# Layer 0 of a four-layer graph network on one core: input loads on one queue, row sums turned by transposes, four index searches moved behind the scaled rows

## The chip, the core and the metric

The kernel runs on 1 core of one Trainium2 chip, as one launch. The metric is device time in microseconds (us): three runs before the change gave a median of 1217.2 us, from 1211.95 to 1225.6. Engines are called PE (matmul), PEld (its weight loads), DVE (vector), ACT (scalar), POOL (GpSimd) and SP (sync, which here only issues transfers). A name with a q behind it, as in SPq, is the sequencer's own work of issuing.

## The reference, cut to what matters

There are 2708 nodes with 128 features `x` and a dense matrix `adj` of 2708 x 2708. Every layer is `x = x + layer(relu(layernorm(x)))`. The change lies in layer 0 (with small consequences in shared helpers):

```python
def layer0(h, A, W1, b1, W2, b2):           # h = relu(layernorm(x)), k = 4
    def lap_mul(A, x):
        d = 1.0 / sqrt(sum(A, axis=-1))     # row sums of A
        return d[:, None] * (A @ (d[:, None] * x))
    z  = leaky_relu(lap_mul(A, h) @ W1 + b1, 0.1)
    sq = sum(z * z, axis=-1)
    d2 = maximum(sq[:, None] + sq[None, :] - 2.0 * (z @ z.T), 0.0)
    S  = exp(-sqrt(d2 + 1e-10) / 2.0)
    S  = where(rank of S in its row < 4, S, 0.0)   # the four nearest nodes
    return lap_mul(S + A, h) @ W2 + b2
```

Layers 1 to 3 are a graph attention (done with a sort and tables), a mean over neighbours, and a plain graph convolution.

## The kernel before, in words

**Tiling.** The nodes lie in T = 22 tiles of 128 rows, the last with 20. `adjT` (the transpose of `adj`) comes from DRAM in 22 chunks of 128 rows x 2708 columns of float32, 1354 KB each; the last has 20 rows (211.6 KB). Columns are handled in six blocks `KBS`: five of 512 and one of 148. `GROUPS` are groups of four tiles, six in all. Chunks 0 to 16 rotate through the four buffers of the pool `big`; chunks 17 to 21 have buffers of their own (`res17` to `res21`) and stay resident between the row sums and the first product of layer 0. The instructions of each engine are put in order by the scheduler of the tile framework, apart from those wrapped in `pin`, which keep the program's order.

**Loads at the start.** ACT's queue loads the nodes `xs` (L85, L86), six weights (L90), three biases spread to all rows (L95), `a_nat` (L105) and stores `order_d` (L137). SP's queue loads the chunks of `adj` (L245). The framework gives the transfers of these hardware queues eight semaphores in turn, so that a transfer also waits for the one that had its semaphore before. The last chunk is loaded four times, to partitions 0, 32, 64 and 96, so that its matmuls with 20 rows can use four row groups of the array.

**Row sums.** As each chunk comes, L355 multiplies it with columns of ones: output in four column groups of 32, six matmuls (twelve instructions of PE, [...]). In between, `weighted` makes `h0 @ W1` and `h0 @ W2` (L323, L334, L341). The sums lie along rows; L372 turns them to one value per partition with 22 matmuls of one column each, and `evacuate` (L149 on DVE, L151 on ACT, in alternation) copies them to `degs`. `inv_sqrt` (L200, L202) makes `dinv`, and L191 scales `y1`.

**First product and z.** `aggregate(y1, to_z)` multiplies all chunks with `y1` (L267) into six PSUM banks `acc0` to `acc5`, the resident chunks last. For each group `to_z` turns the result (L222), makes z (L401, L411), squares it (L414), transposes it to `zT` (L211) and splits -sq/2 into three bf16 parts (L418 to L422), which L427 turns into three rows `sq_rows`.

**Strips.** For each tile t, L463 multiplies z with zT into the six banks, L469 adds the three rows `sq_rows` (a matmul with 3 rows of bf16), and ACT copies the banks to a strip of 128 x 2708 (L472). DVE finds the eight largest of each row (L474, `max`) and their places (L476, `max_index`). Strips use the four buffers of `big`. For the last two tiles the places are searched later, by `find_last` (L490).

**Similarities and second product.** L495, L499 (DVE), a square root and an exponential (L500, L501, ACT) give `sim`; then `find_last(T-2)`, `row_numbers` (L484 to L486), the new row sums (L505, L507), `dinv2` (L200, L202) and the scaled rows `y2` (11 tiles on DVE, L518, 11 on ACT, L516). Two stores write `y2` to `ydr` (L522). `find_last(T-1)` comes last. `aggregate(y2, to_x1)` runs the same products again. Beside it POOL gathers the rows of the four nearest nodes from `ydr` (L539, 88 gathers) and DVE adds them (L545).

Of the kernel before, what the change touches and what calls it, by code (L numbers as in the profile page):

```python
# [18 lines left out]
P = 128  # L19
# [6 lines left out]
def kernel(  # L26
# [44 lines left out]
    ps_a = ctx.enter_context(tc.tile_pool(name="ps_a", bufs=1, space=PSUM))  # L71


    ident = consts.tile([P, P], F32, name="ident")
# [7 lines left out]

    xs = keep.tile([P, T, D], F32, name="xs")
    nc.vector.memset(xs[:, T - 1, :], 0.0)
    nc.scalar.dma_start(xs[:, : T - 1, :], x[: (T - 1) * P, :].rearrange("(t p) f -> p t f", p=P))  # L85
    nc.scalar.dma_start(xs[:TAIL, T - 1, :], x[(T - 1) * P :, :])  # L86

    def load_w(name, w):
        t = consts.tile([P, P], F32, name=name)
        nc.scalar.dma_start(t, w)  # L90
        return t

    def load_b(name, b):
        t = consts.tile([P, P], F32, name=name)
        nc.scalar.dma_start(t, bass.AP(tensor=b.tensor, offset=b.offset, ap=[[0, P], [1, P]]))  # L95
        return t
# [7 lines left out]
    with nc.allow_non_contiguous_dma(reason="256 elements"):  # L104
        nc.scalar.dma_start(  # L105
            a_nat, bass.AP(tensor=l1_a.tensor, offset=l1_a.offset, ap=[[1, P], [P, 2]])
        )
# [28 lines left out]
    nc.vector.memset(nowhere[:, :, 1:2], -1e5)  # L136
    nc.scalar.dma_start(order_d.rearrange("(p t) c -> p t c", t=T), nowhere)  # L137

# [7 lines left out]
    def evacuate(dst, src):  # L146
# [3 lines left out]
        else:  # L150
            nc.scalar.copy(dst, src)  # L151

    def pin(ins):

        return tc.keep_in_program_order(ins)

# [74 lines left out]

    resident = {}
    pools = {}

    def chunk(i):
        if i in resident:
            return resident[i]
        if i >= T - pools["n"]:
            c = resident[i] = pools["res"].tile([P, N + 1], F32, name=f"res{i}")
        else:  # L240
            c = big.tile([P, N + 1], F32, name="chunk", tag="big")

        for g in range(4 if i == T - 1 else 1):
            pin(
                nc.sync.dma_start(  # L245
                    c[32 * g : 32 * g + width(i), :N], adjT[i * P : i * P + width(i), :]
                )
            )
        return c

    def spread(y, queue):

        for g in range(1, 4):
            queue.dma_start(y[32 * g : 32 * g + TAIL, T - 1, :], y[:TAIL, T - 1, :])

    def aggregate(y, done, more=None, kept=0):

        out = [acc(b) for b in range(NKB)]
        last = T - pools["n"]

        def product(i, b):
            k0, n = KBS[b]
            r = slice(32 * (b % 4), 32 * (b % 4) + TAIL) if i == T - 1 else slice(0, P)
            nc.tensor.matmul(  # L267
                out[b][:, :n],
                y[r, i, :],
                chunk(i)[r, k0 : k0 + n],  # L270
                start=(i == 0),
                stop=(i == T - 2),
            )

        for i in range(last):
            if more is not None:
                more(i)
            resident[i] = chunk(i)
            for b in range(NKB):
                product(i, b)  # L280
            if i < last - kept:
                del resident[i]
            if i % 2 and last + i // 2 < T:
                chunk(last + i // 2)
        if more is not None:
            for i in range(last, T):
                more(i)
        for b in range(NKB):
            product(T - 1, b)
        for b in range(NKB):  # L290
            for i in range(last, T - 1):
                product(i, b)
            if b:
                done(b - 1, out)
        done(NKB - 1, out)
# [5 lines left out]

    rows_open = ExitStack()
    res_rows = rows_open.enter_context(tc.tile_pool(name="rows", bufs=1))
    pools.update(res=res_rows, n=L0_RES)
    l0 = ExitStack()
# [42 lines left out]
    for i in range(T):  # L348
# [4 lines left out]
        for b, (k0, n) in enumerate(KBS):  # L353
            g = 32 * (b % 4)
            nc.tensor.matmul(  # L355
                sums[b // 4][g : g + 32, :n],
                ones[:w, :32],
                c[:w, k0 : k0 + n],
                start=(i == 0),
                stop=(i == T - 1),  # L360
            )
    sum_rows = lay.tile([P, 1024], F32, name="sum_rows", tag="U")
    for half, p0, p1 in ((0, 0, 128), (1, 0, 32 * (NKB - 5)), (1, 32 * (NKB - 5), 32 * (NKB - 4))):
        n = KBS[4 * half + p0 // 32][1]
        evacuate(sum_rows[p0:p1, 512 * half : 512 * half + n], sums[half][p0:p1, :n])

    pd = [acc(j) for j in range(4)]
    for b, (t0, t1) in enumerate(GROUPS):
        j = b % 4
        for t in range(t0, t1):  # L370
            o = 512 * (b // 4) + P * (t % 4)
            nc.tensor.matmul(  # L372
                pd[j][: width(t), t : t + 1],
                sum_rows[32 * j : 32 * j + 1, o : o + width(t)],
                ones[32 * j : 32 * j + 1, :1],
                start=True,
                stop=True,
            )
    for b, (t0, t1) in enumerate(GROUPS):
        e = min(t1, T - 1)  # L380
        evacuate(degs[:, t0:e], pd[b % 4][:, t0:e])
    evacuate(degs[:TAIL, T - 1 :], pd[(NG - 1) % 4][:TAIL, T - 1 : T])
    dinv = inv_sqrt("dinv", degs)
# [9 lines left out]

    parts = res.tile([P, T, 3], BF16, name="parts")
    rest = res.tile([P, T, 2], F32, name="rest")
    sq_rows = res.tile([3, N], BF16, name="sq_rows")
    nc.vector.memset(z[:, T - 1, :], 0.0)
# [7 lines left out]
    def to_z(g, s1):  # L405
# [6 lines left out]
        for t in range(t0, t1):  # L412
            junk = small.tile([P, D], F32, name="junk")
            nc.scalar.activation(junk, z[:, t, :], AF.Square, accum_out=sq[:, t, :])  # L414
        transposed(zT, z, g)
        r0, r1, r2 = sq[:, t0:t1, :], rest[:, t0:t1, 0:1], rest[:, t0:t1, 1:2]
        b0, b1_, b2_ = (parts[:, t0:t1, c : c + 1] for c in range(3))
        nc.vector.tensor_scalar(b0, r0, -0.5, None, op0=ALU.mult)  # L418
        nc.vector.scalar_tensor_tensor(r1, r0, -0.5, b0, op0=ALU.mult, op1=ALU.subtract)
        nc.vector.tensor_copy(b1_, r1)  # L420
        nc.vector.tensor_tensor(r2, r1, b1_, ALU.subtract)
        nc.vector.tensor_copy(b2_, r2)  # L422
        p = ps_s.tile([P, 512], F32, name="ps")
        for t in range(t0, t1):
            o = (t - t0) * P
            w = width(t)
            nc.tensor.matmul(  # L427
                p[:3, o : o + w], parts[:w, t, :], ident_b[:w, :w], start=True, stop=True
            )
        evacuate(sq_rows[:, span(g)], p[:3, : span(g).stop - span(g).start])  # L430

# [22 lines left out]
    top_v = res.tile([P, T, 8], F32, name="top_v")  # L454
    top_i = res.tile([P, T, 8], U32, name="top_i")
    strips = []
    nc.vector.memset(top_v[:, T - 1, :], 0.0)
    for t in range(T):
        w = width(t)
        s = big.tile([P, N + 1], F32, name="strip", tag="big")[:, :N]  # L460
        zz = [acc(b) for b in range(NKB)]
        for b, (k0, n) in enumerate(KBS):
            mm = nc.tensor.matmul(  # L463
                zz[b][:w, :n], zT[:, cols(t)], zT[:, k0 : k0 + n], start=True, stop=False
            )
            if t == 1 and b == 0:
                pin(mm)
        for b, (k0, n) in enumerate(KBS):
            nc.tensor.matmul(  # L469
                zz[b][:w, :n], ones_b[:3, :w], sq_rows[:, k0 : k0 + n], start=False, stop=True  # L470
            )
            nc.scalar.copy(s[:w, k0 : k0 + n], zz[b][:w, :n])  # L472
        strips.append(s)
        nc.vector.max(top_v[:w, t, :], s[:w, :])  # L474
        if t < T - 2:
            nc.vector.max_index(top_i[:w, t, :], top_v[:w, t, :], s[:w, :])  # L476


# [20 lines left out]
    pin(nc.vector.tensor_scalar(sim, sim, 0.0, None, op0=ALU.max))  # L499
    nc.scalar.activation(sim, sim, AF.Sqrt, bias=d2_eps)  # L500
    nc.scalar.activation(sim, sim, AF.Exp, scale=-0.5)  # L501
    find_last(T - 2)
    row_numbers(P, 0, T - 1)
    deg2 = small.tile([P, T, 1], F32, name="deg2")
    pin(nc.vector.tensor_reduce(deg2, sim, AX.X, ALU.add))  # L505
    deg2s = small.tile([P, T], F32, name="deg2s")
    pin(nc.vector.tensor_tensor(deg2s, deg2[:, :, 0], degs, ALU.add))  # L507
    dinv2 = inv_sqrt("dinv2", deg2s)
    y2 = lay.tile([P, T, D], F32, name="y2", tag="Y")
# [3 lines left out]
    for t0, t1 in ((0, T // 2), (T // 2, T)):  # L513
        for t in range(t0, t1):
            if t % 2:
                nc.scalar.mul(y2[:, t, :], hw2[:, t, :], dinv2[:, t : t + 1])  # L516
            else:
# [7 lines left out]
        )  # L525
    find_last(T - 1)
    row_numbers(TAIL, T - 1, T)
# [7 lines left out]
    def add_near(t, late=False):  # L535
        w = width(t)
        for k in range(TOPK):
            g = res.tile([P, D], F32, name="gath", bufs=24)
            nc.gpsimd.indirect_dma_start(  # L539
# [760 lines left out]
```

## Time and profile before

| what | us |
|---|---|
| runs, median (lowest to highest) | 1217.2 (1211.95 to 1225.6) |
| the profiled execution | 1218.29 |
| its span | 1216.2 |
| chunk sums end (last L355) | 91.2 from the span's start |
| first matmul of the first product | 97.6 |
| first `max` of the strips | 225.0 |
| last `max` of the strips ends | 347.4 |
| first matmul of the second product | 352.9 |
| layer 0 hands over to layer 1 | about 441 to 482 |

The profile lists, for each engine, what it ran and why it was idle before. A "stage" here is a stretch of the span in microseconds from its start. In the timeline a row is: start, length, engine, line, operation, output<-input, shape, number of merged instructions, and in brackets the idle time before it with what ended that. PE was busy 1054.7 us (87% of the span), DVE 563.8, ACT 407.5, POOL 237.0; the mean granted clock of PE was 0.928. These shares are averages over stages with different limits, so the stages are read one by one.

### The profile page before, as it was taken

Reading aid. Unit: us, or ns where it says so; the run is one execution under the profiler, and the core shown is the slowest. Engines: PE = TensorE matmul, PEld = TensorE weight load, DVE = VectorE, ACT = ScalarE, POOL = GpSimd, SP = SyncE. Lnnn points to the kernel's source line nnn. Section 1 sums busy time; section 2 is a strip of 40 time slices with the busy share of each in tenths; the row PEclk is TensorE's granted clock in tenths of the full one; section 3 lists DMA queues with packets and bytes.
Section 4 is the critical chain, followed back from the end, with each engine's and each line's share of the span. In section 5 each row is a group of like instructions: output and inputs, shape, how many; then the busy total and the mean of one; then the engine's idle time right before and its main releaser. Section 6 shows DMA issues by size and latency. Waiting matters only on the chain.

```text
span 1216.2 us, 10253 instructions
## 1 busy us (share of the span) xinstructions
PE 1054.7 (87%) x3637; PEld 507.0 (42%) x3637; DVE 563.8 (46%) x1172; ACT 407.5 (34%) x643; POOL 237.0 (19%) x200
## 2 busy tenths in 40 slices
PE   4889999999969996977787807777999999999998
PEld 0325444444424445543333303333454455545444
DVE  2001004899972357816666648999720040114003
ACT  3100003444430034767667436878600040003000
POOL 0200000000017773441111035866000000000000
PEclk8998999999989996978989857998889999999999
DMA  8997830000059823869999889999299807753831
GB/s 307 426 359 299 307 133 1 1 0 1 1 218 400 318 53 113 360 222 322 367 380 403 350 351 418 424 424 380 82 383 351 317 33 276 268 184 105 308 136 46
DMA packets 40160, 298.77 MB, mean 246 GB/s; under 512 B 7103, under 2 KB 11214, under 8 KB 13650
## 3 DMA queue, kind: packets, MB, share of 16 engines
q1 hardware_dynamic: 24076, 202.37, 44.3%
q0 software_dynamic: 13600, 93.75, 20.3%
q10 hardware_dynamic: 2434, 2.01, 0.6%
q8 instruction: 29, 0.48, 0.2%
q14 instruction: 21, 0.17, 0.0%
HBM read 265.76 MB, written 32.87 MB: 246 GB/s over the span
## 4 chain that ended last, share of the span: by engine, by line
PE 53%; DVE 20%; DMA 19%; issue 6%; POOL 1%; ACT 1%; SPq 0%; POOLq 0%; DVEq 0%; ACTq 0%
PE acc L267 40%; DMA mov<-in_adj_dram,src_u 7%; DVE top_v L474 5%; DMA chunk<-in_adj_dram 5%; DVE top_i L476 5%; DVE hi L1131 4%; DVE hi L1119 4%; DMA hi<-table,hi_u 2%; DMA res<-in_adj_dram 2%; PE ps L847 2%; PE acc L1036 2%; PE acc L1141 1%; PE ps L224 1%; DMA xs<-in_x_dram 1%; PE ps L355 1%
## 5 line engine op out<-in xcount | busy, mean ns | idle before, releaser
L1141 PE MATMUL acc<-hi,xw 128*128 128x512 f32 (+2 forms) x264 | 119.8, 612 | 63.2 <-DVE hi L1131 63.2
L267 PE MATMUL acc<-chunk,y 128*128 128x512 f32 (+1 forms) x408 | 159.3, 554 | 12.8 <-DVE y L518 10.7
L267 PE MATMUL acc<-chunk,h 128*128 128x512 f32 (+1 forms) x384 | 148.0, 542 | 0.0
L1036 PE MATMUL acc<-mov,wt 128*128 128x512 f32 (+1 forms) x264 | 119.7, 608 | 28.7 <-DMA mov<-in_adj_dram,src_u 28.7
L539 POOL DMA_INDIRECT gath<-ydr,near_u x88 | 84.4, 959 | 284.8 <-DMA ydr<-y 258.3
L267 PEld LDWEIGHTS acc<-chunk,y 128*128 128x128 f32 x408 | 75.0, 194 | 97.1 <-issue 85.6
L463 PE MATMUL acc<-zT 128*128 128x512 f32 (+2 forms) x264 | 108.2, 552 | 1.5 <-ACT strip L472 1.1
L1141 PEld LDWEIGHTS acc<-hi,xw 128*128 128x128 f32 (+1 forms) x264 | 53.7, 212 | 129.1 <-DVE hi L1131 66.7
L1040 DVE COPY mov<-acc 2x512 f32<-2x512 f32 (+1 forms) x126 | 74.6, 612 | 61.0 <-PE acc L1036 59.6
L267 PEld LDWEIGHTS acc<-chunk,h 128*128 128x128 f32 x384 | 68.8, 190 | 74.1 <-issue 74.1
L1036 PEld LDWEIGHTS acc<-mov,wt 128*128 128x128 f32 x264 | 52.5, 210 | 92.0 <-issue 78.0
L472 ACT COPY strip<-acc 128x512 f32<-128x512 f32 (+2 forms) x132 | 60.7, 558 | 73.5 <-issue 58.5
L267 PE MATMUL acc<-chunk,attended 128*128 128x512 f32 x192 | 76.9, 563 | 5.1 <-DMA chunk<-in_adj_dram 5.1
L463 PEld LDWEIGHTS acc<-zT 128*128 128x128 f32 (+1 forms) x264 | 46.4, 185 | 57.3 <-issue 34.1
L1073 POOL DMA_INDIRECT lo<-table,lo_u x22 | 56.0, 2547 | 71.5 <-DVE hi L1119 31.5
L1041 ACT COPY knots<-acc 128x512 f32<-128x512 f32 x88 | 49.9, 586 | 55.7 <-DVE mov L1040 40.0
L1119 DVE SCALAR_TENSOR_TENSOR hi<-lo,lam,hi 128x2708 f32<-128x2708 f32 (+4 forms) x25 | 67.2, 2697 | 1.0
L1123 ACT ACTIVATE hi<-hi,lam 128x2708 f32<-128x2708 f32 (+4 forms) x25 | 56.7, 2280 | 32.5 <-issue 23.4
L1131 DVE SCALAR_TENSOR_TENSOR hi<-row_all,inv_s,hi 128x2708 f32<-128x2708 f32 (+4 forms) x25 | 67.0, 2692 | 0.0
L474 DVE MAX8 top_v<-strip 128x8 f32<-128x2708 f32 (+1 forms) x22 | 64.3, 2963 | 0.2 <-ACT strip L472 0.2
L476 DVE FIND_INDEX8 top_i<-top_v,strip 128x8 uint32<-128x2708 f32 x20 | 59.2, 2972 | 0.0
L545 DVE SCALAR_TENSOR_TENSOR xs<-gath,simd,xs 128x128 f32<-128x128 f32 (+1 forms) x88 | 30.6, 351 | 59.9 <-DMA gath<-ydr,near_u 59.2
(270 smaller groups left out, 1168.1 us busy)
## 6 DMA issues: line engine op xcount, KB each, us to landing
chunk<-in_adj_dram SPq DMA_DIRECT2D x110, 1354.0 KB
table<-knots SPq DMA_DIRECT2D x20, 1354.5 KB
res<-in_adj_dram SPq DMA_DIRECT2D x9, 1354.0 KB
res<-in_adj_dram SPq DMA_DIRECT2D x8, 211.6 KB
ydr<-y SPq DMA_DIRECT2D x2, 704.0 KB
gath<-ydr,near_u POOLq DMA_INDIRECT x88, 5.5
chunkY<-in_adj_dram SPq DMA_DIRECT2D x1, 1354.0 KB
chunkU<-in_adj_dram SPq DMA_DIRECT2D x1, 1354.0 KB
```

The source lines that it names most:

```text
L267: nc.tensor.matmul(out[b][:, :n], y[r, i, :], chunk(i)[r, k0 : k0 + n], start=(i == 0), stop=(i == T - 2),)
L463: mm = nc.tensor.matmul(zz[b][:w, :n], zT[:, cols(t)], zT[:, k0 : k0 + n], start=True, stop=False)
L472: nc.scalar.copy(s[:w, k0 : k0 + n], zz[b][:w, :n])
L474: nc.vector.max(top_v[:w, t, :], s[:w, :])
L476: nc.vector.max_index(top_i[:w, t, :], top_v[:w, t, :], s[:w, :])
L539: nc.gpsimd.indirect_dma_start(out=g[:w, :], out_offset=None, in_=ydr[:, :], in_offset=bass.IndirectOffsetOnAxis(ap=near_u[:w, t, k : k + ...
L1036: nc.tensor.matmul(p[:, :n], wt[:, t, :], moving[t][:, k0 : k0 + n], start=True, stop=True)
L1040: nc.vector.tensor_copy(moving[t + 1][:2, k0 : k0 + n], p[:2, :n])
L1119: nc.vector.scalar_tensor_tensor(num, lo[:w, c], kap, num, op0=ALU.mult, op1=ALU.add)
L1123: nc.scalar.activation(num, num, AF.Ln, scale=sc)
L1131: nc.vector.scalar_tensor_tensor(att[:w, c], row_all[:w, c], inv_s[:w, t : t + 1], att[:w, c], op0=ALU.max, op1=ALU.mult,)
L1141: nc.tensor.matmul(py[b][:, :n], xw[:w, t, :], att[:w, k0 : k0 + n], start=(t == 0), stop=(t == T - 1),)
```

## The change

1. **Loads.** `xs` is loaded first on SP's queue, then chunk 0, the last 20 rows of `xs`, and chunks 1 to 3, and so on. The weights, biases, `a_nat` and `order_d` move from ACT's queue to POOL's. Chunk 21 is loaded once; its three further copies (`last_rows`) follow after four chunks of the first product have been asked for.
2. **Turning the row sums.** The 22 one-column matmuls become ten transposes: four of 128 columns x 128 rows for the first 16 tiles, then four and two on 32 rows. DVE alone copies the results to `degs`, four copies in place of seven.
3. **Squares in four row groups.** The three bf16 parts are written four times, 32 columns apart, so that `sq_rows` holds them at partitions 0, 32, 64 and 96; the 3-row matmul of block b uses row group b % 4, and each tile's blocks go in two batches, four and two.
4. **Index searches.** The searches of tiles 18 and 19 join those of tiles 20 and 21 behind the scaled rows. Strips 18 and 19 use buffers of other tiles (`U` and `Z` of the pool `lay`). `row_numbers` of tiles 0 to 17 comes before the last `max`.
5. **Functions.** The two square roots become exp(0.5 ln) and exp(-0.5 ln); the table of ACT with both is loaded after the copies of tile 4, and the square root's table again after the scaled rows.
6. **Scaled rows.** 13 tiles on DVE, 9 on ACT. The gather buffers go from 24 to 23.

```diff
+    def chunk(i):
...
+        pin(nc.sync.dma_start(c[: width(i), :N], adjT[i * P : i * P + width(i), :]))
+        if i == T - 1:
+            pools["apart"] = True
+        return c
+
+    def last_rows():
+        pools["apart"] = False
+        for g in range(1, 4):
+            pin(
+                nc.sync.dma_start(
+                    resident[T - 1][32 * g : 32 * g + TAIL, :N], adjT[(T - 1) * P :, :]
+                )
+            )
...
+    pin(nc.sync.dma_start(xs[:, : T - 1, :], x[: (T - 1) * P, :].rearrange("(t p) f -> p t f", p=P)))
+    FIRST = 4
+    for i in range(FIRST):
+        resident[i] = chunk(i)
+        if i == 0:
+            pin(nc.sync.dma_start(xs[:TAIL, T - 1, :], x[(T - 1) * P :, :]))
...
-    nc.scalar.dma_start(xs[:, : T - 1, :], x[: (T - 1) * P, :].rearrange("(t p) f -> p t f", p=P))
-    nc.scalar.dma_start(xs[:TAIL, T - 1, :], x[(T - 1) * P :, :])
...
-        nc.scalar.dma_start(t, w)
+        nc.gpsimd.dma_start(t, w)
...
             resident[i] = chunk(i)
+            if i > 2 and T - 1 in resident and pools["apart"]:
+                last_rows()
...
-    pd = [acc(j) for j in range(4)]
-    for b, (t0, t1) in enumerate(GROUPS):
-        j = b % 4
-        for t in range(t0, t1):
-            o = 512 * (b // 4) + P * (t % 4)
-            nc.tensor.matmul(
-                pd[j][: width(t), t : t + 1],
-                sum_rows[32 * j : 32 * j + 1, o : o + width(t)],
-                ones[32 * j : 32 * j + 1, :1],
...
+    for g0, g1 in [(0, 4)] + [(b, b + 1) for b in range(4, NKB)]:
+        pd = acc(max(g0 - 3, 0))
+        r0, r1 = 32 * (g0 % 4), 32 * (g0 % 4 + g1 - g0)
+        e = min(4 * g1, T)
+        for c in range(min(4, e - 4 * g0)):
+            w = min(width(4 * b + c) for b in range(g0, g1))
+            o = 512 * (g0 // 4) + P * c
+            nc.tensor.transpose(
+                pd[:w, P * c : P * c + r1 - r0], sum_rows[r0:r1, o : o + w], ident[r0:r1, r0:r1]
+            )
...
-    sq_rows = res.tile([3, N], BF16, name="sq_rows")
+    sq_rows = res.tile([P, N], BF16, name="sq_rows")
...
+        b0, b1_, b2_ = (part[:, :n, :, c] for c in range(3))
...
+        nc.vector.tensor_scalar(b0, four(r0), -0.5, None, op0=ALU.mult)
...
+    LATE = T - 4
...
+        for bs in (range(4), range(4, NKB)):
+            for b in bs:
+                k0, n = KBS[b]
+                mm = nc.tensor.matmul(
+                    zz[b][:w, :n], zT[:, cols(t)], zT[:, k0 : k0 + n], start=True, stop=False
+                )
...
+            for b in bs:
+                k0, n = KBS[b]
+                g = 32 * (b % 4)
+                nc.tensor.matmul(
+                    zz[b][:w, :n],
+                    ones_b[g : g + 3, :w],
+                    sq_rows[g : g + 3, k0 : k0 + n],
...
-        if t < T - 2:
+        if t < LATE:
             nc.vector.max_index(top_i[:w, t, :], top_v[:w, t, :], s[:w, :])
+        if t == 4:
+            with tc.issue_after(copied.ins):
+                nc.scalar.preload_act_table_set("natural_log_exp_and_others")
...
-    nc.scalar.activation(sim, sim, AF.Sqrt, bias=d2_eps)
+    nc.scalar.activation(sim, sim, AF.Ln, bias=d2_eps)
+    nc.scalar.activation(sim, sim, AF.Exp, scale=0.5)
     nc.scalar.activation(sim, sim, AF.Exp, scale=-0.5)
-    find_last(T - 2)
-    row_numbers(P, 0, T - 1)
+    row_numbers(P, 0, LATE)
...
-    dinv2 = inv_sqrt("dinv2", deg2s)
+    dinv2 = keep.tile([P, T], F32, name="dinv2")
+    nc.scalar.activation(deg2s, deg2s, AF.Ln)
+    nc.scalar.activation(dinv2, deg2s, AF.Exp, scale=-0.5)
...
-            if t % 2:
+            if t % 5 in (1, 3):
...
-    find_last(T - 1)
+    with tc.issue_after(scaled.ins):
+        nc.scalar.preload_act_table_set("sqrt_and_others")
+    for t in (T - 2, T - 1, *range(LATE, T - 2)):
+        find_last(t)
+    row_numbers(P, LATE, T - 1)
     row_numbers(TAIL, T - 1, T)
```

## The prediction

> **What bounds the kernel now.** I read the page's slices first (DMA runs at its height only early, PE later), then the busy times by stage, then inside each stage what ended the last wait. By stage (columns: PE, PEld, DVE, ACT, POOL busy, PE's clock, DMA share, GB/s):
>
> ```profile
> 12.00:15.00 3.00, 1.32 (x12) 0.12 (x2) 0.15 (x1) 0.00 (x0) 0.00 (x0) 1.00 0.96 246
> 27.00:81.00 54.00, 46.79 (x298) 19.14 (x302) 4.20 (x10) 9.65 (x23) 6.16 (x1) 0.97 1.01 424
> 81.00:91.00 10.00, 7.44 (x40) 1.59 (x32) 1.04 (x3) 0.00 (x0) 0.00 (x0) 0.83 1.01 226
> 225.00:342.00 117.00, 116.60 (x354) 51.12 (x353) 117.00 (x61) 53.20 (x118) 0.00 (x0) 1.00 0.02 7
> 342.00:353.00 11.00, 0.35 (x4) 0.09 (x1) 10.50 (x15) 5.99 (x13) 0.00 (x0) 0.66 0.44 186
> ```
>
> The row sums (to 91 us) are bound by DMA: 424 GB/s in mid-stage, but 246 while `xs` and weights come in short rows, and 226 at the end, where the last chunk comes four times. The strips (225 to 342) are bound by DVE, 117.00 us of 117, with PE at 116.60. Then PE waits 11 us. The issues and waits at the start:
>
> ```profile
> 0.82 0.88 SPq L245 DMA_DIRECT2D chunk<-in_adj_dram  x2
> 1.83 9.43 ACTq L86 DMA_DIRECT2D xs<-in_x_dram  x1
> 15.13 1.90 SPq L245 DMA_DIRECT2D chunk<-in_adj_dram  x2
> ...
> SPq L245 <- DMA w<-in_L_gnn_W_dram: 13.4, 1, 13.4
> ```
>
> SP issues two chunks at once and the third only at 15.13: it waits for a weight's transfer, whose semaphore it shares, though its buffer is free. The end of the strips:
>
> ```profile
> 330.35 4.81 PE L463 MATMUL acc<-zT 128*128 128x512 f32 x12
> 335.09 1.31 PE L469 MATMUL acc<-sq_rows,ones_b 3*128 3x512 bf16 x6
> 336.33 4.72 PE L463 MATMUL acc<-zT 128*20 128x512 f32 x12
> 341.44 2.67 ACT L472 COPY strip<-acc 20x512 f32<-20x512 f32 x6 [3.16 <-issue]
> 341.55 5.83 DVE L474 MAX8 top_v<-strip 128x8 f32<-128x2708 f32 x2
> 347.89 2.97 DVE L490 FIND_INDEX8 top_i<-top_v,strip 128x8 uint32<-128x2708 f32 x1
> 348.33 1.28 ACT L501 ACT_TABLE_LOAD   x1
> 349.91 1.28 ACT L200 ACT_TABLE_LOAD   x1
> 352.94 5.54 PE L267 MATMUL acc<-chunk,y 128*128 128x512 f32 x9 [10.65 <-DVE y L518]
> ```
>
> PE makes a strip in 5.98 us (330.35 to 336.33), DVE uses one in 5.83. The last strip is ready at 344.11 and wanted at 344.46: DVE gets no faster here by losing work alone. Then an index search and two table loads stand before the second product.
>
> [...] The trace has such a pack: twelve instructions of 20 rows at L267, 177.82 to 179.73, 1.91 us, against some 4.6 us for twelve of 128 rows. [...]
>
> **The change part by part** (times against the profiled span).
>
> 1. Loads. `xs` is 1.386 MB; first bytes flow at about 2.3 us (the first 3 us moved 0.27 MB). At 246 GB/s it takes 5.6 us, landing near 7.9 instead of 14.85. The eleven small loads, 0.59 MB, cost 2.4 us of DMA [...]. Chunks 0 to 20 are 21 x 1.387 MB at 424 GB/s, 68.7 us. SP no longer waits on weights: in the changed program's list the first wait for a semaphore is with chunk 4, on a transfer landed long before. So chunk 20 lands at 2.3 + 5.6 + 2.4 + 68.7 = 79.0, against 85.83: 6.8 us. Then before, two sums took 85.83 to 91.21, 5.4 us, [...] two take 2 x 1.9 = 3.8 us. End at 82.8, gain 8.4. I take 8.0, since one copy of 20 rows stays. Bounds: 3, if `xs` holds SP as it held ACT's queue (L86, 9.43 us) and transfers pause after it; 10, if short rows run faster alone. POOL's queue: weights stand before its iotas and L385, which was idle 28.8 us before; `w1` is wanted first by L334 at chunk 4. Nothing, unless over 10 us late. The three late copies, 2.8 us at 226 GB/s, stand before chunk 4 of the first product; PE uses 4.6 us a chunk, DMA brings one in 3.27: hidden.
>
> 2. Turning. Before: 91.21 to 97.61, 6.4 us, of which 4.25 in 44 instructions. After: copy of the sums by ACT (0.57), ten transposes (0.66 for four, as at L323, and some 0.6 for the rest), degs copies (0.16 each, two after the last transposes), DVE's 0.30 us copy of the sums' last block, then 0.2 + 0.7 + 0.3 + 0.7 for root, two reciprocals and first scaling, with gaps: 4.2 us. Gain 2.2 (1 to 3).
>
> 3. z stage. Part copies of 16 in place of 4 elements and matmuls 128 wide in place of 3: some 0.1 us a group, as 0.17 us is nearly all fixed cost. Alternation of evacuations flips, with no net load. The first strip gets its last block straight after the last `sq_rows` (in the new order only wg's transposes stand between), where before two L463 and a transpose came first (222.77 to 224.37): gain 1.2 (-1 to 2.5).
>
> 4. Strips. DVE: 22 max and 20 searches took 224.96 to 347.38, 2.915 us each. After: 22 and 18, 116.6, plus `row_numbers` 0.7 ahead of the last max: gain 5.1, if the strips come in time. They need PE below 5.98 - (344.11 - 224.96 - 114.4) / 21 = 5.755 us a strip (114.4 is when the last max is wanted: 39 x 2.915 + 0.7). L463 holds 4.74; two packs of bf16 matmuls cost 2 x 0.21 plus some 0.1 each of start, as the 1.91 us above [...] suggest, against 1.31; and the 0.27 us wait for ACT's first copy goes, as four banks are copied while the other two are filled. Estimate 5.5 (5.2 to 5.9). Strips 18 and 19 have own buffers, so PE is not held.
>
> 5. Chain. Before: 347.38 to y2 at 352.55, 5.2 us. After: 0.5 (L495, L499), ln 0.37, two exp 0.28, reduce and add 0.4, ln and exp 0.22 each, gaps: 2.6. Gain 2.6 (2 to 3). The table loads move beside copies (ACT 53.20 of 117 us busy).
>
> 6. Searches behind. With S the start of y2: DVE scales 13 rows at 0.2 (2.7), then four searches of 3.05: S + 14.9. Queued behind are `row_numbers`, `simd`, the adds L545 at S + 16.2. POOL's first gather waits for ydr and rows 0 to 17 alone (S + 8); at 1.25 us a gather, the 24th, first to need a buffer back, is at S + 36: covered. Chunk 2's load needs strip 20's buffer, free at S + 5.7 (before, issued at S + 3.7); with 3.3 us of transfer [...] it lands near S + 11, and PE wants it at 0.4 + 6.3 + 4.6 = S + 11.3. I charge 0.4 (0 to 2). DVE stays idle 59.9 us beside the gathers, so the adds catch up.
>
> Sum: 8.0 + 2.2 + 1.2 + 5.1 + 2.6 - 0.4 = 18.7 us. Gathers, second product and layers 1 to 3 shift as they are. The profiled execution, 1218.3, becomes 1199.6; it stood 1.1 above the median 1217.2, so the likeliest time is 1199.
>
> **The rivals.** (a) As worked out: 1199, chance 0.68; its own range is 1193 to 1204. (b) Packs don't overlap beside full-width float32: PE stays at 5.98, the last strip comes as before, part 4 gives 0.3: 1204. For: PEld sits idle 0.75 us after the 20-row pack. Against: the pack itself. Chance 0.13. (c) `xs` blocks SP's queue, part 1 gives 3: 1204; together with a late chunk 2, 1206. For: the 9.43 us issue. Against: ACT's queue had to share. Chance 0.11. (d) Slower: each change between full weights and row groups, four a strip, empties the array. Had each pack 0.76 us (the idle time PEld shows before such loads in the z stage), a strip would take 4.74 + 0.63 + 1.52 = 6.89 us, 21 x (6.89 - 5.755) = 24 us late: 1223. It decides from 6.65 us a strip (21 x 0.89 = 18.7). Against: L469 follows L463 today within 0.1 us. Chance 0.04. The remaining 0.04 lies below 1193: more of the first 27 us recovered.
>
> **How the numbers follow.** The range 1191 to 1207 holds (a) to (c). A measurement of this kernel can tell about 1% from no change: faster means under 1205.0. (a), the low rest, and most of (b) and (c): 0.86; within 1%: 0.10; slower 0.04.
>
> **What would show it.** Right: SP issuing chunk 2 in the first microseconds, chunk 20 near 79, L267 from about 87.5; strips at about 5.5 us of PE and DVE without gaps; no table load between the last max and y2, 2.6 us; PE's second product near 334. Wrong: DVE idle for strips; PE idle on chunk 2 after y2; row sums ending past 86.

## The result, and the profile after

The changed kernel takes 1200.5 us (median of 4 runs, 1196.96 to 1212.45); in the same runs the kernel before took 1216.9. The ratio is 0.986, 95% interval 0.982 to 0.991. The forecast was 1199, range 1191 to 1207. The total is right; its parts are not all right, and that their errors have opposite signs, so that the total holds, is luck.

The profiled execution took 1196.96 us, span 1195.2. The same views as of before. First the busy times by stage (columns: PE, PEld, DVE, ACT, POOL busy, PE's clock, DMA share, GB/s):

```profile
12.00:15.00 3.00, 0.00 (x0) 0.00 (x0) 2.27 (x20) 2.66 (x7) 0.00 (x0) 1.00 0.95 238
27.00:78.00 51.00, 44.12 (x291) 17.93 (x291) 3.62 (x6) 5.56 (x10) 2.63 (x1) 1.00 1.01 423
78.00:84.00 6.00, 3.47 (x24) 1.23 (x28) 0.48 (x2) 0.41 (x2) 0.00 (x0) 0.99 1.01 337
216.00:330.00 114.00, 110.56 (x360) 44.86 (x359) 114.00 (x62) 56.79 (x123) 0.00 (x0) 1.00 0.07 25
333.00:336.00 3.00, 0.00 (x0) 0.00 (x0) 1.30 (x6) 1.55 (x6) 0.00 (x0) 0.50 0.00 0
```

The row sums are still bound by DMA at 423 GB/s, and their end is still a slow stretch (337). In the strips DVE is busy without a gap and PE has room. From the end of the last `max` to the second product it is 2.9 us (333.24 to 336.16), where it was 5.6 (347.38 to 352.94); PE itself still waits 9.60 us there, for 10.65 before, since it is done with its strips earlier. Then SP's issues (start, length, engine); among its waits none is for a weight any more:

```profile
0.87 0.90 SPq L114 DMA_DIRECT2D xs<-in_x_dram  x1
1.82 2.83 SPq L87 DMA_DIRECT2D chunk<-in_adj_dram  x1
4.70 0.41 SPq L119 DMA_DIRECT2D xs<-in_x_dram  x1
5.15 33.96 SPq L87 DMA_DIRECT2D chunk<-in_adj_dram  x10
```

And the end of the strips (timeline):

```profile
324.05 5.84 DVE L526 MAX8 top_v<-strip 128x8 f32<-128x2708 f32 x2
325.10 2.67 ACT L524 COPY strip<-acc 20x512 f32<-20x512 f32 x6 [2.76 <-issue]
...
330.28 2.96 DVE L526 MAX8 top_v<-strip 20x8 f32<-20x2708 f32 x1
...
335.31 0.22 ACT L565 ACTIVATE deg2s<-deg2s 128x22 f32<-128x22 f32 x1 [0.53 <-DVE deg2s L563]
335.56 0.22 ACT L566 ACTIVATE dinv<-deg2s 128x22 f32<-128x22 f32 x1
335.81 2.74 ACT L574 ACTIVATE y<-hw,dinv 128x128 f32<-128x128 f32 x9
335.82 2.63 DVE L576 TENSOR_SCALAR y<-hw,dinv 128x128 f32<-128x128 f32 x13 [0.54 <-ACT dinv L566]
336.16 16.42 PE L283 MATMUL acc<-chunk,y 128*128 128x512 f32 x37 [9.60 <-DVE y L576]
```

The last strip is copied at 325.10 + 2.67 = 327.77 and wanted at 330.28; before, it came 0.35 us ahead of its use. Between the last max and the scaled rows there is neither a search nor a table load.

Where the time went, by points that both traces have (us from the span's start; "pack" is where the 20-row matmuls at the end of the first product begin, and the "z stage" runs from there to the first `max`; where an expectation below speaks of the end of that pack, its numbers are counted from this same point):

| point | before | after | gain of the stage | forecast |
|---|---|---|---|---|
| row sums end | 91.21 | 89.31 | 1.9 | 8.0 |
| first scaling of y1 | 96.66 | 91.79 | 3.0 | 2.2 |
| first product starts | 97.61 | 92.59 | 0.2 | - |
| pack | 177.82 | 172.45 | 0.4 | - |
| first max | 224.96 | 215.70 | 3.9 | 1.2 |
| last max ends | 347.38 | 333.24 | 4.9 | 5.1 |
| scaled rows | 352.55 | 335.82 | 2.6 | 2.6 |
| second product starts | 352.94 | 336.16 | 0.0 | -0.4 |

Up to the second product 16.8 us are gained, and the medians differ by 16.4. The profiled span is 21.0 shorter; the further 4.2 lie behind that point, and the profiled execution after is 3.6 below its median, while before's was 1.4 above.

### The profile page after: what moved, and what is told of

The parts are those of the page before. It is cut to its first block, busy times and chain, and to the rows that moved or that the text cites. A ratio compares the mean times of both kernels' runs of the same rounds, so it can differ in the third digit from the quotient of the medians.

```text
span 1195.2 us, 10188 instructions
## 1 busy us (share of the span) xinstructions
PE 1029.7 (86%) x3603; PEld 493.8 (41%) x3603; DVE 561.6 (47%) x1179; ACT 409.8 (34%) x638; POOL 241.9 (20%) x211
## 4 chain that ended last, share of the span: by engine, by line
PE 28%; DMA 13%; DVE 10%; issue 4%; POOL 1%; ACTq 0%; POOLq 0%; DVEq 0%; SPq 0%
PE acc L283 23%; DMA mov<-in_adj_dram,src_u 9%; DVE hi L1193 4%; DVE hi L1181 4%; DMA hi<-table,hi_u 2%; PE acc L1098 2%; PE acc L1203 1%; PE ps L264 1%; DMA chunk<-in_adj_dram 1%; DMA table<-knots 0%; PE ps L262 0%; POOL mov L1012 0%; POOL lo L1135 0%; DVE attended L1233 0%; POOL order_d L876 0%
## 5 line engine op out<-in xcount | busy, mean ns | idle before, releaser
L1203 PE MATMUL acc<-hi,xw 128*128 128x512 f32 (+2 forms) x264 | 117.3, 601 | 64.1 <-DVE hi L1193 64.1
L283 PE MATMUL acc<-chunk,y 128*128 128x512 f32 (+1 forms) x408 | 159.5, 554 | 11.4 <-DVE y L576 9.6
L1098 PE MATMUL acc<-mov,wt 128*128 128x512 f32 (+1 forms) x264 | 117.2, 596 | 32.9 <-DMA mov<-in_adj_dram,src_u 32.9
L509 PE MATMUL acc<-zT 128*128 128x512 f32 (+2 forms) x264 | 112.7, 559 | 0.4 <-ACT strip L524 0.3
L283 PE MATMUL acc<-chunk,attended 128*128 128x512 f32 x192 | 73.1, 542 | 1.2 <-DMA chunk<-in_adj_dram 1.2
L1186 ACT ACTIVATE hi<-hi,hb 128x2708 f32<-128x2708 f32 (+4 forms) x25 | 56.7, 2278 | 0.6
L970 ACT ACTIVATE sg<-row_all,c_nat 128x2708 bf16<-128x2708 f32 (+1 forms) x22 | 56.2, 2553 | 0.1
```

The source lines that it names most:

```text
L283: nc.tensor.matmul(out[b][:, :n], y[r, i, :], chunk(i)[r, k0 : k0 + n], start=(i == 0), stop=(i == T - 2),)
L509: mm = nc.tensor.matmul(zz[b][:w, :n], zT[:, cols(t)], zT[:, k0 : k0 + n], start=True, stop=False)
L1098: nc.tensor.matmul(p[:, :n], wt[:, t, :], moving[t][:, k0 : k0 + n], start=True, stop=True)
L1203: nc.tensor.matmul(py[b][:, :n], xw[:w, t, :], att[:w, k0 : k0 + n], start=(t == 0), stop=(t == T - 1),)
```

## The experiments

All of them but the last two are read from the stages of one profile each, since totals of one kernel differ by a per cent. Eight of these runs came on chips where the kernel before itself took 1304 to 1318 us. The extra time lies behind the start of the second product, and stages ahead of it agree to 0.02 us between chips where they were not edited (z stage 43.24 to 43.26, strips 117.53 or 117.54), so only those stages are compared.

### Strips: packs and late searches, one at a time

```diff
+    sq_rows = res.tile([3, N], BF16, name="sq_rows")
...
+        for bs in (range(NKB),):
...
+                    ones_b[:3, :w],
+                    sq_rows[:, k0 : k0 + n],
```

> The squares as three rows again, added by six K=3 matmuls in a row as before; the four late searches, their buffers and all else as in the changed kernel. Theory (packs are needed for the late searches to pay): PE makes a strip in 5.98 us again, DVE idles for strips, and from the first max to the end of the last it is 122.1 us (the last strip 119.15 after the first max, as before, and one max of 2.97), 4.6 more than the 117.54 of the changed kernel. Rival (PE had room anyway, since DVE alone set the pace): 117.5 to 118.5. On the z stage (end of the first product's 20-row pack to the first max, 47.1 before and 43.25 after): if the packs, with their order of banks, brought its gain, it goes back to 46 or 47; if the order of the evacuations did, it stays within 0.8 of 43.25.

Measured: first max to the end of the last 123.43 us, against 117.54. Timeline of its last strips:

```profile
331.24 1.31 PE L507 MATMUL acc<-sq_rows,ones_b 3*128 3x512 bf16 x6
332.48 4.72 PE L499 MATMUL acc<-zT 128*20 128x512 f32 x12
334.47 2.98 DVE L516 MAX8 top_v<-strip 128x8 f32<-128x2708 f32 x1 [3.05 <-ACT strip L514]
337.13 1.31 PE L507 MATMUL acc<-sq_rows,ones_b 3*20 3x512 bf16 x6
340.29 2.97 DVE L516 MAX8 top_v<-strip 20x8 f32<-20x2708 f32 x1 [2.38 <-ACT strip L514]
```

The brackets are DVE's idle time and what ended it: DVE waits 3.05 us and 2.38 us for ACT's copy, that is for PE. With less work DVE only waits more; moving two searches alone gains nothing. The z stage became 44.48, 1.23 longer: the packs, with their wider parts and their bank order, are worth that there, not the whole 3.9.

```diff
-    LATE = T - 4
+    LATE = T - 2
...
```

> Packs kept; only two searches are put behind the scaled rows, as before, so DVE makes two more before the last max. Theory (DVE sets the pace once the packs are there): first max to end of the last 117.54 + 2 x 2.97 = 123.5 us, DVE busy in all of it, and y2 and the second product 5.9 us later than in the changed kernel (336.16); the gathers' first add is no later than that shift. Rival (PE sets it, near 5.6 us a strip): 119 to 120.

Measured: 122.95 us, DVE busy in all of it:

```profile
213.60:333.50 119.90, 110.80 (x361) 45.04 (x359) 119.90 (x64) 56.78 (x123) 0.00 (x0) 0.98 0.07 24
```

So each half alone leaves the strips at 123 (122.42 before), bound once by PE and once by DVE. Both together gain 4.9.

### z stage: to which engine the copies fall

```diff
+    turn[0] ^= 1
     aggregate(y1, to_z)
```

> The changed kernel with one extra turn of the alternation between DVE and ACT ahead of the first product's results, so that each copy out of PSUM in the z stage goes to the other engine, as it did before. Theory (the z stage gained because of that turn: of the kernel before, DVE's order has the copy of u1T ahead of the leaky relu or of the last part in its slow groups of 6.5 us): 1.5 to 3 us longer from the end of the 20-row pack to the first max, 44.7 to 46.3 in place of 43.25, with two or three groups at 6.2 to 6.5 us. Rival (the gain is of the packs and their bank order): 43.0 to 43.8. The strips and all later stages only shift.

Measured: 46.12 us, 2.9 of the 3.9 lost by one line; the strips took 117.0. DVE in the slow group of this kernel, then in the same group of the changed kernel:

```profile
193.96 1.13 DVE L424 SCALAR_TENSOR_TENSOR z<-ps,dinv,b 128x128 f32<-128x128 f32 x4 [0.94 <-PE ps L262]
195.01 0.68 DVE L193 COPY u1T<-acc 128x512 f32<-128x512 f32 x1
195.60 0.68 DVE L434 SCALAR_TENSOR_TENSOR z<-z 128x512 f32<-128x512 f32 x1
```

```profile
193.16 1.11 DVE L424 SCALAR_TENSOR_TENSOR z<-ps,dinv,b 128x128 f32<-128x128 f32 x4
194.30 0.69 DVE L434 SCALAR_TENSOR_TENSOR z<-z 128x512 f32<-128x512 f32 x1
```

The 0.68 us copy of a later group stands between z and its leaky relu, as in the kernel before at 200.53 us. The chain (z, relu, squares, parts, the next group's z) has no slack: the next group's z comes at 200.19, 6.23 us after this one's, where the changed kernel takes 5.42. But the line moves every copy of the stage, and this one accounts for 0.8 of the 2.9 us: 1.0 more came in the first group and 1.5 between the last group's z and the first `max`, less 0.4 elsewhere. The seven evacuations of the old turning made an odd number, so their removal turned the alternation round for all that follows. 2.9 by the alternation and 1.2 by the packs make 4.1, against 3.9 measured.

### Turning and square roots undone

```diff
+            nc.tensor.matmul(
+                pd[j][: width(t), t : t + 1],
...
+    turn[0] ^= 1
...
+    nc.scalar.activation(sim, sim, AF.Sqrt, bias=d2_eps)
...
+    dinv2 = inv_sqrt("dinv2", deg2s)
...
-                nc.scalar.preload_act_table_set("natural_log_exp_and_others")
```

> Two stages of the changed kernel undone, far from each other: the row sums turned by 22 one-column matmuls and seven copies, as before (with the alternation set so that the z stage keeps its copies), and square roots in place of the logarithms and exponentials, without the early table loads. Theory: from the end of the sums to the first scaling of y1 5.4 us in place of 2.48; from the end of the last max to y2 5.2 us in place of 2.57, with two table loads of 1.28 us between, though no search stands there any more. Rival for the second (the search of tile 20 held the chain, not the tables): 2.6 to 3.5.

Measured: sums' end to the scaling of y1 6.00 us (2.48), and last max to scaled rows 4.41 (2.58). ACT and DVE in the chain:

```profile
333.49 0.37 ACT L551 ACTIVATE sim<-sim,d_eps 128x88 f32<-128x88 f32 x1 [6.03 <-DVE sim L550]
333.88 1.28 ACT L552 ACT_TABLE_LOAD   x1
335.17 0.28 ACT L552 ACTIVATE sim<-sim 128x88 f32<-128x88 f32 x1
335.46 1.28 ACT L240 ACT_TABLE_LOAD   x1
335.48 0.25 DVE L555 TENSOR_REDUCE deg<-sim 128x22 f32<-128x88 f32 x1 [2.02 <-ACT sim L552]
336.76 0.22 ACT L240 ACTIVATE dinv_s<-deg2s 128x22 f32<-128x22 f32 x1
```

Both loads are back and cost 1.83 us. The second overlaps the sum and the add on DVE, so it costs less than its length. The other 0.8 of the 2.6 is what is left of the edits to this chain: the search and `row_numbers` that stood ahead of the row sum. Neither theory had that split.

### Loads: what held chunk 20

The forecast put its landing at 79.0; PE's wait for it ended at 83.91. Were the transfers queued behind it in its way?

```diff
+    gate = resident[T - 2]
+    for i in range(FIRST):
+        c = resident[i] = big.tile([P, N + 1], F32, name="chunk", tag="big")
+        pin(nc.vector.tensor_copy(c[:, 0:1], gate[:, 0:1]))
+        pin(nc.sync.dma_start(c[:, :N], adjT[i * P : (i + 1) * P, :]))
```

> The first product's chunks 0 to 3, and with them the three copies of the last rows, are issued only when chunk 20 of the row sums has landed (four one-column copies on DVE from chunk 20 into their buffers stand in between); otherwise the changed kernel, in which they were issued from 63 us on. Theory (transfers queued behind chunk 20 take a share of the engines, and so it lands some 4 us after its bytes are due): chunk 20 lands at 80 to 81 in place of 83.91, the sums end near 86, and the first product starts near 89.5 in place of 92.59. Rival (the 16 engines are apart by that much whatever is queued behind): chunk 20 lands at 83.4 to 84.2, and the first product starts at 92.5 or later, as chunk 0 comes near 89.5 to 91.

Measured: the wait ended at 83.90, with only the 20 rows of chunk 21 queued behind it. Its last microseconds, in the same columns as above (the last two: DMA share, GB/s):

```profile
79.00:80.00 1.00, 0.41 (x6) 0.16 (x8) 0.00 (x0) 0.41 (x2) 0.00 (x0) 1.00 0.80 260
80.00:81.00 1.00, 1.00 (x11) 0.23 (x4) 0.00 (x0) 0.00 (x0) 0.00 (x0) 1.00 0.52 103
81.00:82.00 1.00, 1.00 (x5) 0.30 (x2) 0.00 (x0) 0.00 (x0) 0.00 (x0) 1.00 0.33 87
82.00:83.00 1.00, 0.43 (x3) 0.12 (x2) 0.48 (x2) 0.00 (x0) 0.00 (x0) 1.00 0.16 65
83.00:84.00 1.00, 0.10 (x4) 0.10 (x8) 0.07 (x1) 0.00 (x0) 0.00 (x0) 1.00 0.05 22
```

This is the rival's picture. The share falls from 0.80 to 0.05 in four microseconds, step by step, and a share of 0.05 is the time of about one engine in 16. The trace also notes completions of each transfer, 16 for a chunk of 128 rows and ten for the 20 rows: chunk 20's came between 79.32 and 83.85 us, and those of the 20 rows behind it between 81.53 and 84.67. So the count's 79 is near chunk 20's first completion, and PE's wait ended 0.05 us after its last: a spread of 4.5 us with hardly anything queued behind. Holding back costs nothing either: chunk 0, issued at 84.15, was there when `y1` was, and the product started at 90.91, ahead of the rival's 92.5.

```diff
-    pin(nc.sync.dma_start(xs[:, : T - 1, :], x[: (T - 1) * P, :].rearrange("(t p) f -> p t f", p=P)))
+    pin(nc.scalar.dma_start(xs[:, : T - 1, :], x[: (T - 1) * P, :].rearrange("(t p) f -> p t f", p=P)))
...
-        nc.gpsimd.dma_start(t, w)
+        nc.scalar.dma_start(t, w)
```

> xs and all eleven small loads on ACT's queue, as before; one copy of the last rows first and three later stays as in the changed kernel. Theory (the gain of the loads is SP's wait for a weight's semaphore, 0.92 MB by 27 us): SP waits past 13 us again with chunk 2, by 27 us some 8.0 MB have moved in place of 8.9, and the sums end near 91.2 in place of 89.31. Rival (the gain is of the last rows' three copies, no longer ahead of the end): the sums end at 89.3 to 89.8.

Measured: SP waits for a weight again, 7.4 MB have moved by 27 us in place of 8.9 (342 and 247 GB/s in 3 to 15 and 15 to 27 us), chunk 17's sum starts at 75.75 and the sums end at 93.08, past the expected 91.2 (the two last ran at half clock for the most part, 6.19 us). From the waits of SP's queue (total, times, longest):

```profile
SPq L87 <- DMA w<-in_L_gnn_W_dram: 13.6, 1, 13.6
```

So with `xs` and the small loads back on ACT's queue the wait is back and the gain of the loads is gone, as forecast; the moved copies of the last rows alone don't bring it. Which of the two moves matters more this run can't say. The `xs` load alone on ACT's queue, the weights left on POOL's:

```diff
-    pin(nc.sync.dma_start(xs[:, : T - 1, :], x[: (T - 1) * P, :].rearrange("(t p) f -> p t f", p=P)))
+    pin(nc.scalar.dma_start(xs[:, : T - 1, :], x[: (T - 1) * P, :].rearrange("(t p) f -> p t f", p=P)))
...
```

> xs goes back to ACT's queue and the weights stay on GpSimd's; SP issues chunks 0 to 3 at once, nothing ahead of them. Theory (what stands ahead of chunk 20 is a number of bytes, and it is the same): the sums end within 0.7 us of 89.31. Rival A (xs alone in a queue moves at 246 GB/s, so beside chunks the first 15 us move more): the sums end 1 to 2.5 us earlier. Rival B (short rows and chunks on two queues disturb each other, or a shared semaphore holds SP): 1 to 2 us later.

Measured: the sums end at 97.82, 8.5 later; rival B had the direction, none the size. The waits up to 40 us, and one of SP's queue:

```profile
DVE ln_st L211 <- DMA xs<-in_x_dram: 28.3, 1, 28.3
PE acc L338 <- ACT h L221: 11.4, 1, 11.4
SPq L87 <- DMA xs<-in_x_dram: 13.7, 1, 13.7
```

With four chunks at once beside it `xs` lands late: DVE waits for it until 30.7 us, and SP too holds a chunk back for 13.7 us until then, since that chunk has `xs`'s semaphore. The normalised rows come late, PE stands 11.4 us on their transposes in the middle of the row sums, chunks' buffers aren't freed, and DMA moves 327 GB/s in 27 to 78 us. So the small loads' move to POOL's queue gained nothing with `xs` on ACT's (97.82, against 93.08 in `act_queue`); a count of bytes can't see that. The other half, `xs` on SP's queue with the small loads left on ACT's, was not run.

```diff
+        if name in ("w1", "w2"):
+            nc.gpsimd.dma_start(t, w)
+        else:
+            late.append((t, w))
...
+    pin(nc.gpsimd.tensor_copy(gate, resident[T - 2][:, 0:1]))
+    for t_, src in late:
+        pin(nc.gpsimd.dma_start(t_, src))
```

> Seven of the eleven small loads (wg, ws, wn, w3, b1, b2, b3, 0.46 MB) are issued on GpSimd's queue only after chunk 20 has landed; w1, w2, a_nat and order_d stay. Theory (they cost the row sums their bytes, 1.1 us at 424 GB/s, or 1.9 at the 246 GB/s of short rows): the sums of chunk 17 start 1.1 to 1.9 us earlier than the 72.3 to 72.8 of the changed kernel and three like it, and the sums' end moves by as much against a mean of 88.5 over five runs, within their spread of 3 us. They then run beside the first product, which stays at 79.6 to 80.2 us. Rival (in the first 15 us the loads take only what xs and the chunks leave free): chunk 17 at 72 to 73 as before.

Measured: chunk 17's sum starts at 69.17; in the eight runs with the small loads first in POOL's queue and the chunks in order it was 70.88 to 73.31, mean 72.25. That is 3.1 us for 0.46 MB, more than the estimate: in 3 to 15 us the DMA moved 364 GB/s in place of 308 to 341 in these eight, which suggests that the small rows also slow what runs beside them. The sums end at 84.01, the earliest of all. But the first product then took 82.58 us in place of 79.9, and half of the gain or more was gone by the pack (169.86, against 172.45 and 170.69 in the changed kernel's two profiles). Its start at half clock is no more than the changed kernel's; new is a wait for a chunk:

```profile
110.63 14.73 PE L288 MATMUL acc<-chunk,y 128*128 128x512 f32 x38 [2.29 <-DMA chunk<-in_adj_dram]
```

The small loads now run beside the first product's chunks: DMA moved 278 GB/s in 88 to 92 us, where the changed kernel's second profile has 425. So their cost may in part only have been moved.

### The two last sums and PE's clock

```diff
-    for i in range(T):
+    for j, i in enumerate([*range(T - 2), T - 1, T - 2]):
...
```

> The 20 rows of the last chunk are loaded and summed ahead of chunk 20, so that only one chunk's sum is left when it lands; all else as in the changed kernel. Theory (the last landing plus a slow-clock sum sets the end): chunk 20 lands at 83.9 to 84.4, one sum of some 2.7 us follows in place of 5.40, the sums end at 86.8 to 87.2 in place of 89.31 and the first product starts near 90.2 in place of 92.59. Rival (the clock, low after the wait, makes the first sum alone take over 4 us, or the 20 rows ahead delay chunk 20 by a microsecond and more): the first product starts at 91.5 to 92.6.

Measured: the sums end at 87.41, the first product starts at 90.69, the clock stays full, and the first product takes 78.06 us. Here chunk 19, not 20, was late (81.10), so PE ran 21 and 20 in one go of 3.73 us without a wait: near the expected end, though not by the expected way.

By then two last sums had taken 3.73 to 3.90 us after waits up to 1.74 us and 5.38 to 7.17 after 1.94 us and more, and I took a wait of 1.9 us for the cause.

```diff
+        if i == T - 2:
+            idle = acc(2)
+            for _ in range(4):
+                pin(nc.tensor.matmul(idle[:32, :], ones[:, :32], prev[:, :512], start=True, stop=True))
...
+    idle = acc(4)
+    for _ in range(4):
+        pin(nc.tensor.matmul(idle[:32, :], ones[:, :32], prev[:, :512], start=True, stop=True))
```

> The changed kernel with matmuls whose product nobody reads, four on PE just ahead of chunk 20's sum and four behind the ten transposes, 1.3 us each time at full clock, so that PE is not idle long there. Theory (a wait of PE of about 1.9 us or more halves the clock granted for the next microseconds: the two last sums took 3.73 to 3.90 us after waits of 1.47 to 1.74 us, and 5.38 to 7.17 after waits of 1.94 to 2.93): from chunk 20's first sum to the end 3.7 to 3.9 us whenever it lands, and from the first product's first matmul to its 20-row pack 78.1 us, as in the one run whose clock stayed full, in place of 79.6 to 80.2. Rival (the slow stretch is bound to the time or to the sums, not to the wait): 5.4 and 79.9 as in the changed kernel.

Measured: the sums ran from 83.72 to 88.29, 4.6 us, the first beside the last idle matmul. The first product ran 77.4 us, but it started at 95.04, since the second four matmuls took 5.3 us in place of 1.3. The theory falls twice over. In the ten microseconds before, PE had no pause of even one, and the clock was halved from 90.4 to 93.8 all the same. And the changed kernel, run again, waited 2.28 us and kept the clock (timeline of PE), where its first profile waited 1.94 us and lost it, as `flip` did after the same 2.28 us:

```profile
83.25 1.90 PE L370 MATMUL ps<-res,ones 128*32 128x512 f32 x12 [2.28 <-DMA res<-in_adj_dram]
```

```profile
83.91 5.40 PE L370 MATMUL ps<-res,ones 128*32 128x512 f32 x24 [1.94 <-DMA res<-in_adj_dram]
```

```profile
83.77 5.38 PE L370 MATMUL ps<-res,ones 128*32 128x512 f32 x24 [2.28 <-DMA res<-in_adj_dram]
```

The clock of that first profile by microseconds (column before the DMA share):

```profile
82.00:83.00 1.00, 0.00 (x0) 0.00 (x0) 0.48 (x2) 0.00 (x0) 0.00 (x0) 1.00 0.98 379
83.00:84.00 1.00, 0.09 (x4) 0.09 (x8) 0.00 (x0) 0.00 (x0) 0.00 (x0) 0.94 1.07 363
84.00:86.00 2.00, 2.00 (x11) 0.47 (x12) 0.00 (x0) 0.00 (x0) 0.00 (x0) 0.50 1.00 401
86.00:87.00 1.00, 1.00 (x4) 0.00 (x0) 0.00 (x0) 0.00 (x0) 0.00 (x0) 0.50 0.92 390
87.00:88.00 1.00, 1.00 (x9) 0.27 (x10) 0.00 (x0) 0.00 (x0) 0.00 (x0) 0.85 1.05 444
```

Half clock lasts from 83.89 to 87.30, 3.41 us in the trace's record of the granted clock. In each of thirteen profiles, all but that of the three edits below, the changes of clock stand whole multiples of 3.41 us apart. Here are the 3.41 us ahead of such a point, in the changed kernel's first profile, in `flip` and in the second profile:

```profile
80.48:83.89 3.41, 1.49 (x8) 0.41 (x4) 0.48 (x2) 0.00 (x0) 0.00 (x0) 1.00 1.00 345
80.86:84.27 3.41, 1.13 (x12) 0.43 (x14) 0.48 (x2) 0.00 (x0) 0.00 (x0) 1.00 0.95 276
81.99:85.40 3.41, 1.90 (x12) 0.39 (x12) 0.00 (x0) 0.00 (x0) 0.00 (x0) 1.00 1.01 310
```

PE was busy 1.49 and 1.13 us and half clock followed; with 1.90 us the clock stayed full, though the wait was as long as in `flip`. The thirteen profiles show the same. Of their 1173 such windows from 20 to 330 us, the 53 that half clock followed held at most 1.49 us of matmuls with 128 rows (time at half clock counted half), the other 1120 at least 1.33. Matmuls with fewer rows don't seem to count: in `warm`'s window from 86.97 to 90.38 PE was busy 3.14 us, but 1.15 us with 128 rows. So up to 330 us half clock goes with little work in such a window, and not with the length of the wait; it was read afterwards, no run tested it, and behind 330 us 31 of 711 windows with half clock after them don't fit.

### Three edits together

```diff
+    for j, i in enumerate([*range(T - 2), T - 1, T - 2]):
...
+            for _ in range(2):
...
+            late.append((t, w))
```

> Three edits to the changed kernel together: the 20 rows loaded and summed ahead of chunk 20, the seven small loads after it, and idle matmuls in both gaps of PE (two and four). Theory: one sum of 1.9 us after the last landing near 83, so the sums end at 85 to 86.5 in place of 89.31, the first product takes 78.1 us, and the second product starts at 329.5 to 331 in place of 336.16, some 5 to 6 us earlier; median 5 us below the changed kernel's in the same call, ratio to the kernel before near 0.982. Rival (the end of the loads and its spread between engines set the end whatever is done): 0 to 2 us below.

> The changed kernel itself once more, as the base for the three edits on the same chip and for the spread of its front. Ratio to the kernel before 0.986 as measured first; the sums' end between 85.6 and 91.6 us, as in five runs with these loads; z stage 43.26 us, first max to the end of the last 117.53 us, last max to y2 2.58 us, as in every run that left them alone.

These two ran side by side on one chip. The three edits (`rows_first`, `late_w`, and idle matmuls, two and four): ratio to the kernel before 0.982, interval 0.979 to 0.985. The changed kernel: 0.9864, 0.9822 to 0.9906. The direction is the expected one, at about 4 us of 1290, but the intervals overlap: it isn't shown that the three beat the change. The one profile of the three edits caught an execution of 2160 us, with about 1.03 us for a matmul, so their stages were not seen. In its second profile the changed kernel had the sums' end at 87.60, z stage 43.25, strips 117.54, last max to scaled rows 2.58, and the second product at 334.40.

## Why the prediction was right, and where it was not

**The sum.** 18.7 us were forecast to the second product; 16.8 and 18.5 were measured in two profiles after, against the one before. The total holds since one step was 6 us too high and two others together 3.5 too low.

**Part 1 failed, at "So chunk 20 lands at 79.0, against 85.83: 6.8 us."** The count of bytes was right: 8.9 MB by 27 us against 9.06 by that count. But 79.0 is near the first of chunk 20's 16 completions (79.25 in the profile after), and 85.83 was a measured landing, just behind the last. A modelled time was compared with a measured one, and the 4.2 us between the first completion and the last came out as a gain: chunk 20's completions ran from 81.57 to 85.78 before and from 79.25 to 83.87 after, so like compared with like the gain is 2.3 or 1.9 us. The wait for chunk 20 ended between 81.67 and 84.41 in seven profiles with these loads, mean 83.4. The second term, "two take 2 x 1.9", holds only where the clock does (3.73 to 3.90), and it was 5.38 to 7.17 where the clock fell (before, to 0.50 from 86.2 to 89.6 us); that the clock would hold was the author's estimate. The sums' end was 85.57 to 91.58 in the seven, mean 88.2, which is 3.0 ahead of the one profile before: the lower bound that the prediction gave, but for another reason than the one it named there, since `xs` did not hold SP.

**Part 2, turning:** 3.0 for 2.2, the upper bound; undone, it cost 3.5, of which some 0.6 is PE's half clock in that run (4.81 us for the 44 instructions, 4.25 before).

**Part 3 failed at "Alternation of evacuations flips, with no net load."** The load is nearly the same (the copies of parts took 0.17 us with 4 elements and 0.20 with 16); the order of each engine's copies is not, and it is worth 2.9 us. The 1.2 us charged to the earlier last block equal the 1.23 of the packs and their bank order by luck. The step that they were charged to, from the last group's z to the first `max`, took 6.27 us before (218.69 to 224.96), 6.28 in `flip`, 5.05 in `three_rows` and 4.77 after: it too goes mostly with the alternation.

**Part 4** was right in size (4.9 for 5.1) and in its mechanism: neither half alone gains. PE's strips came 5.58 us apart (304.35, 309.93, 315.52 us), for an estimate of 5.5 and a limit of 5.755. Rival (b), no overlap of packs, and (d), an emptied array, are gone: four 3-row matmuls took 0.40 us (from 302.40) beside full-width float32, where six in one row group took 1.31 before.

**Part 5** had the right 2.6 but didn't say what it is of: 1.83 go with the table loads, 0.8 with the search and `row_numbers`. Ln and Exp run in turn from 333.80 to 335.78 with no load between them.

**Part 6:** the charge of 0.4 fell away. The second product runs 37 instructions without a stall from 336.16: chunk 2, issued at 341.48, had landed at 347.23, 11.4 us after the scaling began, where 11 was forecast. The first gather came 7.3 us after the scaling began and the first add 15.1, for 8 and 16.2 forecast.

## What to carry to other kernels

When a landing is forecast from a rate, compare it with a rate's landing before, or carry the measured lag over: chunk 20's last completion came 3.1 to 5.3 us after its first in the seven profiles. Where a helper alternates between engines, an edit upstream that removes an odd number of calls re-deals all that follows; read the order of the chain's own engine before calling it no net load. Of two engines that both filled a stage here (122.42 us), relieving one gained nothing (123.43 and 122.95) and relieving both gained 4.9, so price such edits as a pair.

## What the runs showed of the hardware that was not expected

- One transfer's 16 completions came over 4.5 us (79.32 to 83.85, `hold`) with only 20 rows queued behind, and over 4.6 (79.25 to 83.87, the changed kernel) with whole chunks behind.
- Half clock came in stretches of 3.41 us or a multiple (83.9 to 87.3; 90.4 to 93.8), and the wait before didn't tell when (after 2.28 us it came in `flip` and not in the changed kernel's second profile): from 20 to 330 us the windows of 3.41 us that it followed held at most 1.49 us of 128-row matmuls.
- Column groups matter much: six 32-column float32 matmuls over four groups took 1.90 us; four into one group took about 3.4 at full clock (`warm`, from 81.14), 0.86 each against 0.32, where the expectation had 1.3 for the four.
- Seven small loads of 0.46 MB cost the row sums 3.1 us up to chunk 17 (one run against the mean of eight, which spread over 2.4), where their bytes at 424 GB/s are 1.1.
